# Projecting later images two units at a time: v's products 512 columns wide, q's and k's in longer runs

## The chip, the core and the metric

One Trainium2 chip, one core. The metric is the time of one launch on the device in microseconds, the median of several runs. The profile is of one further execution.

## The reference

A self-attention layer over each of 4 images of 64 x 64 places with 256 channels, in fp32:

```
N = W * H                                   # 4096
q = x Wq + bq    (128 channels)
k = x Wk + bk    (128 channels)
v = x Wv + bv    (256 channels)
pq = q.reshape(B, -1, N); pk = ...; pv = ...   # reshape, not transpose
energy = einsum('bcn,bcm->bnm', pq, pk)
attention = softmax(energy)
out = einsum('bcm,bnm->bcn', pv, attention).reshape(B, W, H, C)
return gamma * out + x
```

## The kernel before

TensorE multiplies in fp32r, and each operand is split into forms: an upper part `h`, the rest `l`, and a form `d` that makes up for the cross terms. A product is therefore three matmuls (forms 0, 1, 2) into one or two accumulators.

**Image 0** is projected at the start, unit by unit (16 units of 256 places). **The main loop** then runs over 512 steps `n`: 4 images x 8 groups (of 512 rows of the attention) x 16 steps `t` (of 256 columns each). In step `n` TensorE's instructions are laid out by hand, in this order:

- `cross(n + 2)`: two 512-column matmuls (L331), which ScalarE rescales in place (L332, "muls");
- `attend(n, 0)`: six 512-column matmuls (L403) into the accumulators `a0`, `b0`;
- `energy(n + 2)`: four matmuls (L346), followed by ScalarE's exponentials (L349) and its upper forms `h` (L355, in `upper`);
- a piece of the projection of the *next* image (`step(p, "pe")`);
- in the first step of a group, `sums`: two matmuls `z` (L441) for the softmax's sums of the group before;
- `attend(n, 1)`: six matmuls (L403) into `a1`, `b1`.

VectorE makes in each step the sum of the exponentials (L366) and the forms `l` and `d` (L380, L382, in `halves`). At a group's end `emptied` has ScalarE copy the accumulators into the tile `o` (L417): those of half 0 in the last step (t = 15), those of half 1 in the first step of the next group (t = 0), after that step's exponentials. `attend(n, 1)` of t = 0 starts to fill `a1` again, so it comes behind that copy. In the last image, which has no projection beside it, half 1 is emptied one step later (`late`) and two more PSUM banks are used.

`finish` ends a group in twelve pieces, one for each step (`proceed`): the sums go through DRAM and a reciprocal and come back as `r`, VectorE adds the two parts of `o` at t = 4 and multiplies by `r` at t = 7, GpSimd's queue adds `x` by DMA from t = 8, and SP's queue stores the result from t = 11.

The projection of the next image goes along in `step(p, engine)`, where `p` counts its own steps: `p = n - 4` at first, two of them in each step from n = 16 to 23, then `p = n + 4`. A unit has R = 8 steps `r`: transposes at r = 0 (four, L207), x's forms at 1 and 2 (L218, L220, L222), q's and k's products at r = 3 (four 256-column matmuls, L238) and 4 (eight), v's at 5 (four) and 6 (eight), the forms between and behind them (L260, L267, L278, L281, L155, L158). They use two PSUM banks in turn, which `z` uses too. The finished forms are stored to DRAM by SP's queue (`store`, L302), and come back by GpSimd's queue: `load_k` in every step, `load_v` for each of 16 steps around the change to the next image (768 KB each).

The SBUF pool `work` has tiles by tag: `xin` (one buffer) for the loaded x (`load_x`, L199), `xf` (one) for x's forms, `pf` (two in turn) for the forms of q, k and v until they are stored, `r` (one) for `zf` and `r`, `o` (one).

Of the kernel before, what the change touches and what calls it, by code (L numbers as in the profile page):

```python
# [9 lines left out]
F32 = mybir.dt.float32  # L10
F32R = mybir.dt.float32r
I32 = mybir.dt.int32
AF = mybir.ActivationFunctionType
# [7 lines left out]
def kernel(  # L21
# [36 lines left out]
    nc = tc.nc  # L58
    B, W, H, C = x.shape
    P = 128  # L60
# [3 lines left out]
    KC = C // P  # L64
    NI = NM // 2
# [9 lines left out]
    XB = 256  # L75
    xv = columns(x, XB)
# [4 lines left out]
    REST = 1.0 / (1.0 + E)  # L81
    NB = 512
    NJ = NB // P
    NG = N // NB
    NU = NM // 2
# [15 lines left out]
    with ExitStack() as fast:  # L101
# [22 lines left out]
        nc.scalar.dma_start(raw[:, 0, :, C2:], wk.rearrange("(k p) d -> p k d", p=P))  # L124
        nc.sync.dma_start(raw[:, 1], wv.rearrange("(k p) e -> p k e", p=P))
        nc.gpsimd.memset(zs, 1.0)
        bf = work.tile([P, 3, KC, 2, P], F32R, tag="xf", name="bf", bufs=1)
        bf = bf[:, 0, 0].rearrange("p s a -> p (s a)")
        rows = work.tile([P, 2, XB], F32, tag="xin", name="rows", bufs=1)[:33, 0]
        nc.vector.memset(rows, 0.0)  # L130
        for eh in range(KC):
            nc.gpsimd.dma_start(bvs[:, eh : eh + 1], bv[eh * P : (eh + 1) * P].unsqueeze(1))
# [56 lines left out]
            return pool.tile(shape, F32, tag=tag, name=name)  # L189

        def load_x(b, i):
            if i >= NI:
                return
            if b == 0:
                t = xs4[:, i % 4]
            else:
                t = work.tile([P, 2, XB], F32, tag="xin", name=f"x_{b}_{i}", bufs=1)
            if b or i:
                nc.sync.dma_start(t, xv[b, i])  # L199
            loads["x", b, i] = t  # L200

        def transposed(b, i):
            xs = loads.pop(("x", b, i))
# [5 lines left out]
        def x_forms(b, i):  # L209

            y = units.pop(("xt", b, i))
            if b == 0:
                f = ppool.tile([P, 3, KC, 2, P], F32R, tag="ld", name=f"xf_{b}_{i}")
            else:
                f = work.tile([P, 3, KC, 2, P], F32R, tag="xf", name=f"xf_{b}_{i}", bufs=1)
            units["xf", b, i] = f
            h = f[:, 0]
            nc.scalar.activation(h, y, AF.Identity, scale=UPPER)  # L218
            yield
            nc.vector.scalar_tensor_tensor(f[:, 2], h.bitcast(F32), 1.0 + E, y, ALU.mult, ALU.subtract)  # L220
            yield
            nc.vector.tensor_tensor(f[:, 1], y, h.bitcast(F32), ALU.subtract)  # L222
            yield

        def products(b, i, w, fs):
# [5 lines left out]
            for s in range(2):  # L231
                for f in fs:
                    for k in range(KC):
# [10 lines left out]
                            skip_group_check=True,  # L244
                        )

        def biased(i):

            to = units[0, 0, i]
            for s in range(2):  # L250
                nc.tensor.matmul(  # L251
                    to[:, s, :], ones_r, bf, start=False, stop=True, skip_group_check=True,
                )

        def seed_qk(b, i):
            y = units[0, b, i]
            if b == 0:
                nc.scalar.activation(y, y, AF.Identity, scale=REST)
                return
            nc.vector.scalar_tensor_tensor(  # L260
                y, y, REST, bias.unsqueeze(1).to_broadcast([P, 2, C]), ALU.mult, ALU.add
            )

        def seed_v(b, i):
            y = units[1, b, i]
            for eh in range(KC):
                nc.scalar.activation(  # L267
                    y[:, eh, :], y[:, eh, :], AF.Identity, bias=bvs[:, eh : eh + 1], scale=REST
                )

        def qk_forms(b, i):
            y = units.pop((0, b, i)).rearrange("p s (w a) -> p s w a", w=2)
# [13 lines left out]
                stores.append((kf[b, i // 2 + NU // 2 * s][:, i % 2], f[:, s, 1]))  # L286
                stores.append((qd[b, i // NJ + NG // 2 * s][:, i % NJ], f[:, s, 0]))

        def v_forms(b, i):
            y = units.pop((1, b, i))  # L290
            units.pop(("xf", b, i))
            if b == 0:
                f = vall[:, i]
            else:
                f = work.tile([P, 3, 2, C], F32R, tag="pf", name=f"vf_{b}_{i}")
            yield from split(f[:, 0], f[:, 1], f[:, 2], y)
            if b:
                stores.append((vf[b, i], f))

        def store():  # L300
            for to, f in stores:
# [122 lines left out]
        def sum_forms(n):  # L424

            s = now["total"] = now["sum"]
            f = work.tile([P, 2, NB], F32R, tag="r", name=f"zf_{n // NU}", bufs=1)
            h, l = now["z"] = f[:, 0, :], f[:, 1, :]
            nc.scalar.activation(h, s[:, 0, :], AF.Identity, scale=UPPER)
            yield  # L430
            nc.vector.tensor_tensor(l, s[:, 0, :], h.bitcast(F32), ALU.subtract)
            yield
# [11 lines left out]
        def finish(n, o, s):  # L444
            b, g = divmod(n, NG)
            r4 = rall[:, n, :]
            row = lambda t: t[n : n + 1, :]
            spread = lambda t: row(t).rearrange("o (p j) -> (o p) j", j=NJ)
            nc.sync.dma_start(row(zd), s[0:1, 0, :])
            yield  # L450
            nc.sync.dma_start(r4, spread(zd))
            yield
            yield
            nc.vector.reciprocal(r4, r4)
            yield
            nc.sync.dma_start(spread(rd), r4)
            nc.vector.tensor_tensor(o[:, 0], o[:, 0], o[:, 1], ALU.add)
            yield
            r = work.tile([P, NB], F32, tag="r", name=f"r_{n}", bufs=1)
            nc.sync.dma_start(r, rd[n, :].partition_broadcast(P))  # L460
            yield
            yield
            nc.vector.tensor_tensor(
                o[:, 0], o[:, 0], r.unsqueeze(1).to_broadcast([P, 2, NB]), ALU.mult
            )
            yield
            nc.gpsimd.dma_start(o[:, 0], xg[b, g], accum_op=ALU.add)
            yield
            yield
            yield  # L470
            nc.sync.dma_start(og[b, g], o[:, 0])
# [6 lines left out]
        def finish_last(n, xr):  # L478

            b, g = B - 1, NG - 1  # L480
            S = now["sum"][:, 0, :]
            f = work.tile([P, 2, NB], F32R, tag="r", name="zf_last", bufs=1)
            nc.scalar.activation(f[:, 0, :], S, AF.Identity, scale=UPPER)
            nc.vector.tensor_tensor(f[:, 1, :], S, f[:, 0, :].bitcast(F32), ALU.subtract)
            attend(n, 0)
# [41 lines left out]
            nc.sync.dma_start(og[b, g][:, 1], xr[:, 1, :])  # L527


        R = STEPS // NI  # L530

        def step(n, engine):

            if n < 0:
                return
            b, u = divmod(n, STEPS)
            i, r = divmod(u, R)
            b += 1
            made = now["made"]
            if engine == "pe" and b < B:  # L540
                if r == 0:
                    transposed(b, i)
                elif r == 3:
                    products(b, i, 0, (2,))
                elif r == 4:
                    products(b, i, 0, (0, 1))
                elif r == 5:
                    products(b, i, 1, (2,))
                elif r == 6:
                    products(b, i, 1, (0, 1))  # L550
            elif engine == "act" and b < B:
                if r == 1:
                    made["x"] = x_forms(b, i)
                    next(made["x"])
                    load_x(b, i + 1)
                elif r == 5:
                    made["qk"] = qk_forms(b, i)
                    next(made["qk"])
                elif r == 6:
                    seed_v(b, i)  # L560
                elif r == 7:
                    made["v"] = v_forms(b, i)
                    next(made["v"])
            elif engine == "dve":
                if r == 0 and "v" in made:
                    for _ in made.pop("v"):
                        pass
                if b < B:
                    if r in (1, 2):
                        next(made["x"])  # L570
                    elif r == 3:
                        seed_qk(b, i)
                    elif r == 5:
                        next(made["qk"])
                    elif r == 6:
                        for _ in made.pop("qk"):
                            pass
                    elif r == 7:
                        next(made["v"])

        now["made"] = {}
        now["turn"], now["banks"] = 0, [(ps_p, "p0"), (ps_p, "p1")]
# [32 lines left out]
        for i in range(NI):  # L615
# [3 lines left out]
            next(qk)  # L619
            if i == 0:  # L620
                products(0, 0, 1, (2,))
                seed_v(0, 0)
                products(0, 1, 0, (2,))
                seed_qk(0, 1)
            products(0, i, 1, (0, 1))
            vs = v_forms(0, i)
            next(vs)
            xs = iter(())
            if i + 1 < NI:
                if i:  # L630
                    products(0, i + 1, 0, (2,))
                    seed_qk(0, i + 1)
                products(0, i + 1, 1, (2,))
                seed_v(0, i + 1)
            if i + 2 < NI:
                transposed(0, i + 2)
                xs = x_forms(0, i + 2)
# [20 lines left out]
        for n in range(B * STEPS):  # L658
# [5 lines left out]
                load_x(1, 0)  # L664
            if u == STEPS - 5 and b + 2 < B:
                image(b + 2)
                load_x(b + 2, 0)
            if n == B * STEPS - 6:
                xr = ppool.tile([P, 2, NB], F32, tag="s", name="xr")
                nc.sync.dma_start(xr, xg[b, g])  # L670
# [4 lines left out]
            if turn:  # L675
                zf = sum_forms(n)
                next(zf)
            p = n - 4 if n < 16 else 2 * n - 20 if n < 24 else n + 4
            step(p, "act")
            if not final:  # L680
                attend(n, 0)
# [22 lines left out]
                break  # L704
            attend(n, 1)
            full = now["a", 1], now["b", 1]
            if 16 <= n < 24:
                for engine in ("act", "pe", "dve"):
                    step(p + 1, engine)
            if t == 6 and n + NU < B * STEPS:  # L710
# [221 lines left out]
```

## Time and profile before

| | |
|---|---|
| median of 3 runs | 2358.28 us (2358.22 to 2358.36) |
| the profiled execution | 2358.95 us, its span 2357.1 us |
| granted TensorE clock | 0.999 |
| busy: TensorE / VectorE / ScalarE | 99% / 91% / 80% |
| DMA | 413.82 MB, mean 176 GB/s |
| one group of 16 steps, images 0 to 2 | 72.8 us |

PE is TensorE's matmul, PEld its weight load, DVE VectorE, ACT ScalarE, POOL GpSimd, SP the queue of stores and of x's loads. Busy times of single matmuls overlap. `out<-in` names the tiles that an instruction writes and reads; a note in brackets tells how long the engine was idle before it and what released it.

### The profile page before, as it was taken

The numbers are of one execution on the slowest core, as the hardware profiler recorded it, in microseconds if no ns is written. First come the engines' busy times: TensorE is split into PE (matmuls) and PEld (weight loads), VectorE is DVE, ScalarE is ACT, GpSimd is POOL, SyncE is SP. The second block draws the span as 40 slices with busy tenths as digits, with TensorE's granted clock in tenths as the row PEclk, the third lists the DMA queues.
The fourth block names the chain that finished last, engine by engine and source line by source line (L and its number), as shares of the span: only waits on it lengthen the run. The fifth ranks groups of instructions, "written<-read, shape, count | busy, mean of one in ns | idle before, by whom it ended". The sixth has DMA issues, their size and how long they took to land.

```text
span 2357.1 us, 32019 instructions
## 1 busy us (share of the span) xinstructions
PE 2343.1 (99%) x11132; PEld 1958.5 (83%) x11132; DVE 2135.7 (91%) x2114; ACT 1878.8 (80%) x3090; POOL 355.7 (15%) x642
## 2 busy tenths in 40 slices
PE   9999999999999999999999999999999999999998
PEld 9888888888888888888888888888888888888886
DVE  8989999989999899999999999999989888888888
ACT  7788778888788887888878888778887777888785
POOL 1111111111211111111121111111112111111110
PEclk9999999999999999999999999999999999999999
DMA  8556665556975556556597555665559554444443
GB/s 281 153 161 176 177 172 159 166 158 175 305 240 173 149 174 188 162 159 165 154 344 223 161 166 157 178 173 159 172 152 353 159 134 121 121 130 118 130 130 96
DMA packets 178894, 413.82 MB, mean 176 GB/s; under 512 B 26083, under 2 KB 76519, under 8 KB 178726
## 3 DMA queue, kind: packets, MB, share of 16 engines
q0 software_dynamic: 94272, 280.67, 45.4%
q1 hardware_dynamic: 83902, 130.77, 15.4%
q8 instruction: 91, 1.49, 0.3%
q14 instruction: 77, 0.63, 0.1%
q10 hardware_dynamic: 552, 0.26, 0.0%
HBM read 306.64 MB, written 104.98 MB: 175 GB/s over the span
## 4 chain that ended last, share of the span: by engine, by line
PE 97%; ACT 1%; DVE 1%; issue 0%; DMA 0%; POOL 0%; ACTq 0%; DVEq 0%; POOLq 0%; SPq 0%
PE a L403 39%; PE e L346 20%; PE b L403 19%; PE e L331 10%; PE qv L238 7%; PE xt L207 1%; PE z L441 1%; ACT x L349 0%; ACT o L417 0%; DMA bias<-in_L_conv_bk_dram 0%; ACT e L332 0%; DVE f L281 0%; ACT h L355 0%; PE qv L251 0%; DVE v L158 0%
## 5 line engine op out<-in xcount | busy, mean ns | idle before, releaser
L349 ACT ACTIVATE x<-e 128x512 f32<-128x512 f32 x960 | 522.1, 596 | 295.5 <-PE e L346 289.0
L366 DVE TENSOR_TENSOR s<-s,x 128x1024 f32<-128x1024 f32 x480 | 586.7, 1222 | 94.6 <-ACT x L349 92.1
L380 DVE TENSOR_TENSOR ld<-x,h 128x1024 fp32r<-128x1024 f32 x480 | 586.3, 1221 | 87.3 <-ACT h L355 57.8
L403 PE MATMUL a<-h,v 128*128 128x512 f32 x2048 | 641.0, 394 | 0.0
L332 ACT ACTIVATE e<-e 128x512 f32<-128x512 f32 x1024 | 546.8, 573 | 109.1 <-PE e L331 108.7
L403 PE MATMUL a<-ld,v 128*128 128x512 f32 x2048 | 632.8, 390 | 0.0
L403 PE MATMUL b<-ld,v 128*128 128x512 f32 x2048 | 631.7, 390 | 0.2
L382 DVE SCALAR_TENSOR_TENSOR ld<-h,x 128x1024 fp32r<-128x1024 f32 x480 | 584.9, 1219 | 0.0
L318 POOL DMA_DIRECT2D k<-kf x512 | 272.1, 531 | 1942.4 <-PE e L346 1826.2
L346 PE MATMUL e<-q,k 128*128 128x512 f32 x2048 | 548.8, 390 | 1.1
L355 ACT ACTIVATE h<-x 128x1024 fp32r<-128x1024 f32 x480 | 510.6, 1064 | 13.2
L403 PEld LDWEIGHTS a<-ld,v 128*128 128x128 f32 x2048 | 384.4, 188 | 83.2
L403 PEld LDWEIGHTS b<-ld,v 128*128 128x128 f32 x2048 | 384.1, 188 | 83.5 <-DVE ld L382 1.0
L346 PEld LDWEIGHTS e<-q,k 128*128 128x128 f32 x2048 | 383.0, 188 | 84.5 <-ACT e L332 6.0
L403 PEld LDWEIGHTS a<-h,v 128*128 128x128 f32 x2048 | 368.6, 189 | 69.4 <-ACT o L417 7.3
L331 PE MATMUL e<-q,k 128*128 128x512 f32 x1024 | 316.1, 390 | 0.0
L331 PEld LDWEIGHTS e<-q,k 128*128 128x128 f32 x1024 | 191.7, 188 | 40.5
L238 PEld LDWEIGHTS qv<-wf,xf 128*128 128x128 f32 x768 | 108.5, 193 | 10.7 <-DVE xf L220 1.8
L238 PE MATMUL qv<-wf,xf 128*128 128x256 f32 x768 | 115.3, 287 | 1.6 <-DVE xf L220 1.4
L238 PEld LDWEIGHTS qv<-xf,wf 128*128 128x128 f32 x768 | 107.1, 191 | 8.6 <-ACT s L442 0.7
L238 PE MATMUL qv<-xf,wf 128*128 128x256 f32 x768 | 112.6, 283 | 0.5 <-ACT s L442 0.3
L281 DVE SCALAR_TENSOR_TENSOR f<-f,qv 128x512 fp32r<-128x512 f32 x128 | 85.8, 681 | 3.6 <-ACT f L278 3.1
(83 smaller groups left out, 1006.6 us busy)
## 6 DMA issues: line engine op xcount, KB each, us to landing
k<-kf POOLq DMA_DIRECT2D x512, 384.0 KB, 3.6
vf<-vf SPq DMA_DIRECT2D x48, 768.0 KB
v<-vf POOLq DMA_DIRECT2D x48, 768.0 KB, 8.1
kf<-f SPq DMA_DIRECT2D x128, 192.0 KB
qd<-f SPq DMA_DIRECT2D x128, 192.0 KB
q<-qd POOLq DMA_DIRECT2D x31, 768.0 KB, 4.8
o<-in_x_dram POOLq DMA_DIRECT2D x31, 512.0 KB, 7.3
out_dram<-o SPq DMA_DIRECT2D x31, 512.0 KB
```

The lines of the kernel that those rows point to most:

```text
L238: nc.tensor.matmul(to[:, s, :], left, right.rearrange("p s a -> p (s a)") if w else right, start=(f == 2 and s == k == 0), stop=(f == 1 an ...
L281: nc.vector.scalar_tensor_tensor(f[:, :, :, j, :], h.bitcast(F32), s, y, ALU.mult, op)
L318: nc.gpsimd.dma_start(t, kf[b, u % NU])
L331: nc.tensor.matmul(e, *forms(n, i, 2), start=True, stop=False, skip_group_check=True)
L332: nc.scalar.mul(e, e, -REST)
L346: nc.tensor.matmul(e, *forms(n, i, f), start=False, stop=(f == 1), skip_group_check=True)
L349: nc.scalar.activation(x[:, i, :], e, AF.Exp, scale=(1.0 + E) ** 3 / E)
L355: nc.scalar.activation(h, units[n], AF.Identity, scale=UPPER)
L366: nc.vector.tensor_tensor(s, s, x, ALU.add)
L380: nc.vector.tensor_tensor(l, x, h.bitcast(F32), ALU.subtract)
L382: nc.vector.scalar_tensor_tensor(d, h.bitcast(F32), 1.0 + E, x, ALU.mult, ALU.subtract)
L403: nc.tensor.matmul(to, vall[:, t, f, i, j * P : (j + 1) * P], units[n][f][:, i, :], start=(t == 0 and i == 0 and f != 1), stop=(t == NU - ...
```

## The change

Images 1 to 3 are projected by pairs of units. R becomes 16 steps per pair, and the steps are laid out anew:

- r = 0: the transposes of both units (eight); r = 1 to 4: x's forms of both, written side by side into one `xf` tile of double size;
- r = 5: the first four products of q and k of both units; r = 6: the other eight of both; their seeds on VectorE at r = 5, their forms at r = 7 to 10;
- r = 9 and 10: v's products of the first half of the channels, for both units at once, 512 columns wide (`products_v`: two matmuls at r = 9, four at r = 10); r = 11 and 12: the second half; seeds on ScalarE at r = 10 and 12, one of 512 columns each (`seed_v_pair`), forms at r = 11 to 14 (`v_pair_forms`), each stored with two DMAs;
- r = 15: both units of the next pair of x are loaded, with two DMAs.

`p = n - 3` at first, two of them in each step from n = 17 to 22, then `p = n + 3`. The tags `xin` and `r` go: the pair of x and `zf` take places in the ring `pf`, and `r` is loaded into the half of `o` that is free by then. The main loop's other calls stand as they were.

```diff
         def load_x(b, i):
...
+            pair = work.tile([P, 2, 2, XB], F32, tag="pf", name=f"x_{b}_{i}")
+            for u in range(2):
+                nc.sync.dma_start(pair[:, u], xv[b, i + u])
+                loads["x", b, i + u] = pair[:, u]
...
+        def products_v(b, i, eh, fs):
+            xf = units["xp", b, i]
+            if fs[0] == 2:
+                units["v", b, i, eh] = bank(f"v{eh}_{b}_{i}", [P, 2, C], b, 1)
+            to = units["v", b, i, eh]
+            for f in fs:
+                for k in range(KC):
+                    nc.tensor.matmul(
+                        to.rearrange("p u c -> p (u c)"),
+                        wf[:, 1, f, k, eh * P : (eh + 1) * P],
+                        xf[:, f, k].rearrange("p u s a -> p (u s a)"),
+                        start=(f == 2 and k == 0),
+                        stop=(f == 1 and k == KC - 1),
+                        skip_group_check=True,
+                    )
...
+        def seed_v_pair(b, i, eh):
+            y = units["v", b, i, eh]
+            nc.scalar.activation(y, y, AF.Identity, bias=bvs[:, eh : eh + 1], scale=REST)
...
+        def v_pair_forms(b, i, eh):
+            y = units.pop(("v", b, i, eh))
+            f = work.tile([P, 3, 2, C], F32R, tag="pf", name=f"vf{eh}_{b}_{i}")
             yield from split(f[:, 0], f[:, 1], f[:, 2], y)
+            for u in range(2):
+                stores.append((vf[b, i + u][:, :, eh, :], f[:, :, u, :]))
...
-            f = work.tile([P, 2, NB], F32R, tag="r", name=f"zf_{n // NU}", bufs=1)
+            f = work.tile([P, 2, NB], F32R, tag="pf", name=f"zf_{n // NU}")
...
-            r = work.tile([P, NB], F32, tag="r", name=f"r_{n}", bufs=1)
+            r = o[:, 1, 0]
...
-        R = STEPS // NI
+        R = 2 * STEPS // NI
...
+            if engine == "pe":
                 if r == 0:
                     transposed(b, i)
-                elif r == 3:
+                    transposed(b, i + 1)
+                elif r == 5:
                     products(b, i, 0, (2,))
-                elif r == 4:
+                    products(b, i + 1, 0, (2,))
+                elif r == 6:
                     products(b, i, 0, (0, 1))
+                    products(b, i + 1, 0, (0, 1))
+                elif r in (9, 11):
+                    products_v(b, i, r // 11, (2,))
+                elif r in (10, 12):
+                    products_v(b, i, r // 12, (0, 1))
+            elif engine == "act":
+                if r in (1, 2):
+                    begin(("x", r - 1), x_forms(b, i + r - 1))
+                elif r in (7, 8):
+                    begin(("qk", r - 7), qk_forms(b, i + r - 7))
+                elif r in (10, 12):
+                    seed_v_pair(b, i, r // 12)
+                elif r in (11, 13):
+                    begin(("v", r // 13), v_pair_forms(b, i, r // 13))
+                elif r == 15:
+                    load_x(b + (i + 2) // NI, (i + 2) % NI)
+            else:
+                if 1 <= r <= 4:
+                    next(made["x", (r - 1) // 2])
                 elif r == 5:
...
+                elif 7 <= r <= 10:
+                    next(made["qk", (r - 7) // 2])
...
+                elif 11 <= r <= 14:
+                    next(made["v", (r - 11) // 2])
...
-            p = n - 4 if n < 16 else 2 * n - 20 if n < 24 else n + 4
+            p = n - 3 if n < 17 else 2 * n - 20 if n < 23 else n + 3
...
-            if 16 <= n < 24:
+            if 17 <= n < 23:
                 for engine in ("act", "pe", "dve"):
                     step(p + 1, engine)
```

More of the change, by code (lines that the diff above doesn't have):

```diff
@@ L126 @@
         nc.gpsimd.memset(zs, 1.0)
-        bf = work.tile([P, 3, KC, 2, P], F32R, tag="xf", name="bf", bufs=1)
-        bf = bf[:, 0, 0].rearrange("p s a -> p (s a)")
-        rows = work.tile([P, 2, XB], F32, tag="xin", name="rows", bufs=1)[:33, 0]
+        bf = work.tile([P, 3, KC, 2, 2, P], F32R, tag="xf", name="bf", bufs=1)
+        bf = bf[:, 0, 0, 0].rearrange("p s a -> p (s a)")
+        rows = work.tile([P, 2, XB], F32, tag="pf", name="rows")[:33, 0]
         nc.vector.memset(rows, 0.0)
@@ L191, in load_x @@
         def load_x(b, i):
-            if i >= NI:
+            if b == B or i >= NI:
                 return
@@ L195, in load_x @@
                 t = xs4[:, i % 4]
[L196 to L200, printed above, removed]
+                if i:
+                    nc.sync.dma_start(t, xv[b, i])
+                loads["x", b, i] = t
+                return
+            pair = work.tile([P, 2, 2, XB], F32, tag="pf", name=f"x_{b}_{i}")
+            for u in range(2):
+                nc.sync.dma_start(pair[:, u], xv[b, i + u])
+                loads["x", b, i + u] = pair[:, u]
         def transposed(b, i):
@@ L213, in x_forms @@
                 f = ppool.tile([P, 3, KC, 2, P], F32R, tag="ld", name=f"xf_{b}_{i}")
+            elif i % 2 == 0:
+                f = units["xp", b, i] = work.tile(
+                    [P, 3, KC, 2, 2, P], F32R, tag="xf", name=f"xf_{b}_{i}", bufs=1
+                )
+                f = f[:, :, :, 0]
             else:
-                f = work.tile([P, 3, KC, 2, P], F32R, tag="xf", name=f"xf_{b}_{i}", bufs=1)
+                f = units["xp", b, i - 1][:, :, :, 1]
             units["xf", b, i] = f
@@ L245, in products @@
                         )
+        def products_v(b, i, eh, fs):
[12 more added lines that the diff above has]
+                        skip_group_check=True,
+                    )
         def biased(i):
@@ L262, in seed_qk, with seed_v @@
             )
-        def seed_v(b, i):
-            y = units[1, b, i]
+        def seed_v(i):
+            y = units[1, 0, i]
             for eh in range(KC):
@@ L287, in qk_forms, with v_forms @@
                 stores.append((qd[b, i // NJ + NG // 2 * s][:, i % NJ], f[:, s, 0]))
[L289 to L295, printed above, removed]
+        def v_forms(i):
+            y = units.pop((1, 0, i))
+            units.pop(("xf", 0, i))
+            yield from split(vall[:, i, 0], vall[:, i, 1], vall[:, i, 2], y)
+        def v_pair_forms(b, i, eh):
+            y = units.pop(("v", b, i, eh))
+            f = work.tile([P, 3, 2, C], F32R, tag="pf", name=f"vf{eh}_{b}_{i}")
             yield from split(f[:, 0], f[:, 1], f[:, 2], y)
-            if b:
-                stores.append((vf[b, i], f))
+            for u in range(2):
+                stores.append((vf[b, i + u][:, :, eh, :], f[:, :, u, :]))
         def store():
@@ L481, in finish_last @@
             S = now["sum"][:, 0, :]
-            f = work.tile([P, 2, NB], F32R, tag="r", name="zf_last", bufs=1)
+            f = work.tile([P, 2, NB], F32R, tag="pf", name="zf_last")
             nc.scalar.activation(f[:, 0, :], S, AF.Identity, scale=UPPER)
@@ L537, in step, with begin @@
             i, r = divmod(u, R)
-            b += 1
+            b, i = b + 1, 2 * i
+            if b >= B:
+                return
             made = now["made"]
-            if engine == "pe" and b < B:
+            def begin(key, pieces):
+                made[key] = pieces
+                next(pieces)
+            if engine == "pe":
                 if r == 0:
                     transposed(b, i)
-                elif r == 3:
+                    transposed(b, i + 1)
+                elif r == 5:
@@ L544, in step @@
                     products(b, i, 0, (2,))
-                elif r == 4:
+                    products(b, i + 1, 0, (2,))
+                elif r == 6:
                     products(b, i, 0, (0, 1))
-                elif r == 5:
[L548 to L579, printed above, removed]
@@ new lines, in step @@
+                    products(b, i + 1, 0, (0, 1))
[17 more added lines that the diff above has]
+                    next(made["x", (r - 1) // 2])
+                elif r == 5:
+                    seed_qk(b, i)
+                    seed_qk(b, i + 1)
+                elif 7 <= r <= 10:
+                    next(made["qk", (r - 7) // 2])
+                    if r % 2 == 0:
+                        next(made["qk", (r - 7) // 2], None)
+                elif 11 <= r <= 14:
+                    next(made["v", (r - 11) // 2])
+                    if r % 2 == 0:
+                        next(made["v", (r - 11) // 2], None)
@@ L621 @@
                 products(0, 0, 1, (2,))
-                seed_v(0, 0)
+                seed_v(0)
                 products(0, 1, 0, (2,))
@@ L625 @@
             products(0, i, 1, (0, 1))
-            vs = v_forms(0, i)
+            vs = v_forms(i)
             next(vs)
@@ L633 @@
                 products(0, i + 1, 1, (2,))
-                seed_v(0, i + 1)
+                seed_v(i + 1)
             if i + 2 < NI:
@@ L666 @@
                 image(b + 2)
-                load_x(b + 2, 0)
             if n == B * STEPS - 6:
```

## The prediction

> **What bounds the kernel now.** I read the page first: busy times, then the chain that ended last.
>
> ```profile
> span 2357.1 us, 32019 instructions
> PE 2343.1 (99%) x11132; PEld 1958.5 (83%) x11132; DVE 2135.7 (91%) x2114; ACT 1878.8 (80%) x3090; POOL 355.7 (15%) x642
> PE 97%; ACT 1%; DVE 1%; issue 0%; DMA 0%; POOL 0%; ACTq 0%; DVEq 0%; POOLq 0%; SPq 0%
> L403 PEld LDWEIGHTS a<-h,v 128*128 128x128 f32 x2048 | 368.6, 189 | 69.4 <-ACT o L417 7.3
> ```
>
> TensorE is the bound from end to end, so a change pays only if it shortens TensorE's stream or its waits, and every new wait of TensorE is paid in full. The last line is the one to remember: weight loads of the attention products sat idle until ScalarE's copies out of the accumulators (L417) had ended, 7.3 us in all. The list of that line's waits says 23 times, 0.32 us each: once at nearly every group start. The timeline of one such start (step 48, whose `cross` begins at 290.55):
>
> ```profile
> 287.78 1.07 PE L346 MATMUL e<-q,k 128*128 128x512 f32 x4
> 288.43 1.09 ACT L349 ACTIVATE x<-e 128x512 f32<-128x512 f32 x2 [0.38 <-PE e L346]
> 289.97 0.70 ACT L417 ACTIVATE o<-b,gam 128x512 f32<-128x512 f32 x1
> 290.55 0.61 PE L331 MATMUL e<-q,k 128*128 128x512 f32 x2
> 290.97 1.07 ACT L332 ACTIVATE e<-e 128x512 f32<-128x512 f32 x2 [0.30 <-PE e L331]
> 292.36 1.07 PE L346 MATMUL e<-q,k 128*128 128x512 f32 x4
> 293.01 1.09 ACT L349 ACTIVATE x<-e 128x512 f32<-128x512 f32 x2
> 293.27 1.11 PE L238 MATMUL qv<-wf,xf 128*128 128x256 f32 x8
> 293.98 0.69 ACT L417 ACTIVATE o<-a,gam 128x512 f32<-128x512 f32 x1
> 294.22 0.63 PE L441 MATMUL z<-zf,ones 128*128 128x512 f32 x2
> 294.73 0.30 PEld L403 LDWEIGHTS a<-h,v 128*128 128x128 f32 x2 [0.32 <-ACT o L417]
> 295.30 0.62 PE L403 MATMUL a<-ld,v 128*128 128x512 f32 x2
> ```
>
> Busy times overlap (matmuls are pipelined), so I take start to start. Four 512-column matmuls take 0.91 us (292.36 to 293.27): 0.2275 each. Eight 256-column ones take 0.95 (293.27 to 294.22): 0.119 each. The second accumulator half `a1` can be written only when the copy that began at 293.98 has ended at 294.67. TensorE would have been there at 294.68 and, because the weight load also waited, its next pair began at 295.30 where 295.13 was due: 0.17 us paid. What nearly hides the copies is the eight projection products (0.95) and `z` (0.46) between `energy` and `attend(n, 1)`.
>
> **The change, part by part.**
>
> *v's products.* In images 1 to 3, 48 units x 12 products of 256 columns become 288 of 512. Each saves 2 x 0.119 - 0.2275 = 0.010 us: 2.9 us. (With single intervals from the trace, 120 and 227 ns, 13 ns and 3.7 us.) The Trainium skill, "TensorE: Matmul & The Clock Gate", section "Wait — 56ns, not 53.3ns?", puts the fixed cost of a warm matmul at about 2.5 ns. By that the merging would bring an estimated 288 x 2.5 ns = 0.7 us and the sum below would end 2.2 us higher; this trace shows 10 to 13 ns, and goes ahead of it.
>
> *Longer runs.* Four transposes and the return to attention products take 0.44 + 0.03 us in the chain (the row after them lasts 0.94, not 0.91). Two runs joined save that return once, about 0.03 x 24 = 0.8 us. Runs of q's and k's products show no such step (120 ns to the last), so joining them brings nothing. Part sum -3.7, bounds -2.9 and -5.
>
> *ScalarE and VectorE.* VectorE has the same 14 pieces per pair (0.61 us start to start, beside 3 x 1.135 in each step). The hand-set steps bunch them: two seeds in one step, `o`'s addition and multiplication beside q's and k's forms. I followed its lag through one group: at worst 2 us, and TensorE asks for `d` about 1.7 us after that; hidden, and with that cover gone it would be TensorE's wait. ScalarE has two seeds of 512 columns instead of four of 256 (0.47 each): less work, off the bound.
>
> *The phase.* This is the large term. Before, step p = n + 4 of units of 8 puts eight products (r = 4) into every group's first step (t = 0) and four (r = 3) into the last. After, p = n + 3 of pairs of 16 puts t = 0 at r = 3, where TensorE has nothing to project, and t = 15 at r = 2, where TensorE has nothing either but ScalarE an x form more. The order of the built programs agrees: `energy`, the two `z` matmuls, `a1`. So at t = 0 the eight products no longer cover the copies. From the rows above: the last step is 0.48 shorter, so `cross` starts at 290.07. ScalarE's added x form (0.55 start to start) eats the 0.38 idle ahead of the exponentials, which start 0.10 late; half 0's copies end 290.77 with the next operation possible at 290.65, so L332 starts 0.16 later than TensorE would let it. From L332's start to the copy's it is 3.01 us (290.97 to 293.98), all back to back: copy from 293.66 to 294.35, weight load at 294.41, next pair 0.57 later (as 294.73 to 295.30): 294.98. TensorE's due time: 290.07 + 0.455 + 1.36 + 0.91 + 0.455 for the `a1` pair is 293.25, and 293.70 for the next. Paid: 1.28, against 0.17: 1.11 us more per group start. The groups that begin at n = 32, 48, ..., 368 are 22: **+24.4 us**. Lower bound: the exponentials are held by TensorE alone (second one ready 0.42 after the last `energy` start, as at 288.43): 0.87 each, 19.1. Upper: the x form finds no idle time and delays all by 0.39 more: 1.5 each, 33.0. I take the middle because the 0.38 of idle is in the row.
>
> *The start n = 16* falls on r = 13. There ScalarE must make v's `h` (L155) between L332 and the exponentials, in a `pf` buffer whose last store (first half of v) was made by VectorE only one step earlier, since `zf` now takes a place in the same ring of two. Store issue 0.5 each and some 4.5 us to land (the packets of v's store at 157.6 ended 4.2 after issue): about 2 us of wait plus 0.55, so 3.5 more, once; bounds 1 and 5.
>
> *SP's queue.* The pair of x is loaded at r = 15, one step before its transposes (before: seven steps), into the buffer that held the first half of v. The load waits in SP's queue for those stores, and behind `out`'s; v's second stores wait behind it. In an ordinary group: VectorE ends the piece 4 us into r = 12, stores land near 10, `out` is queued at 7, x lands at 12.5 to 15.5 (x's packets end 4.2 to 4.9 us after issue); the transposes come at 19.8. Hidden by 4 us. But at the turn to images 2 and 3 `load_v` fills the DMA engines:
>
> ```profile
> 620.00:640.00 20.00, 20.00 (x99) 16.84 (x99) 18.22 (x18) 14.88 (x25) 5.43 (x9) 1.00 1.09 342
> 640.61 0.55 SPq L199 DMA_DIRECT2D x<-in_x_dram  x1
> ```
>
> The DMA share is 1.09, and the x load of 640.61 had its last packet 8.0 us after issue, `out`'s at 633.6 11.3 us. With v's stores ahead x lands 22 to 23 us after r = 12 began: about 2.5 us late, twice: **+5**, bounds 0 and 12. v's stores in 1 KB runs instead of 6 KB cost the DMA engines 6 x 46 ns instead of 234; hidden outside those stretches.
>
> *Sum.* The profiled execution took 2358.95 us, 0.67 over the median of the runs. 2358.95 - 3.7 + 24.4 + 3.5 + 5 = 2388.2; less 0.67: **2387.5 us**.
>
> **Rivals.** (1) *The copies hide.* If the releaser named in that row is wrong, or ScalarE reaches the copies early enough that `a1` waits no longer than now, only the first term is left: 2358.3 - 3.7 = 2354.6, faster. It decides from 0.16 us more per start: below that, 23 waits cost less than 3.7. For it: TensorE's merged work is real. Against: 294.73 follows the copy's end by 0.06 us, 23 times over. (2) *x late at each pair.* If stores and `out` together take 6 us longer than I put, transposes wait 2 us at all 24 pairs: 48 more, about 2435. For it: one step of lead instead of seven. Against: margins of 4 us from measured landings. (3) *A draw*: rival 1 with waits of some 0.2 us, near 2358.
>
> **How the numbers follow.** Forecast 0.84, rival 1 0.05, rival 2 0.08, rival 3 0.03. The range takes in the forecast's bounds: 2358.3 + 19.1 + 1 - 5 = 2373 and 2358.3 + 33 + 5 + 12 - 2.9 = 2405, which would all have to fall together; I give 2372 to 2403, leaving the other cases out. A measurement tells 0.2% (4.7 us) from no change. Slower holds the forecast and rival 2: 0.92; same 0.03; faster 0.05.
>
> **What would show it.** In the changed profile the weight loads `a<-h,v` waiting for `o` should sum to some 25 to 35 us instead of 7.3, 23 times; the chain should show a piece of ScalarE at each group start 72 to 73 us apart. v's products should stand 0.227 apart. Transposes waiting for x should show at the two image turns only. I am wrong if a group (16 steps) from n = 32 on is not about 1 us longer than now.

## The result, and the profile after

The changed kernel takes 2398.39 us (median of 6 runs, 2396.61 to 2399.51), the kernel before 2358.43 beside it: ratio 1.0169, 95% interval 1.0158 to 1.018, some 40 us slower. The prediction was 2387.5, range 2372 to 2403. The profiled execution took 2396.61 us; its span is 37.6 us longer than that of before.

The page of the changed kernel, in answer to the four lines shown of before (lines move: 403 is now 433, 417 is 447, 331 is 361, 346 is 376, 441 is 471, 199 is 202):

```profile
span 2394.7 us, 31637 instructions
PE 2342.7 (98%) x10844; PEld 1948.1 (81%) x10844; DVE 2124.7 (89%) x2114; ACT 1858.6 (78%) x3042; POOL 355.8 (15%) x642
PE 86%; ACT 10%; DMA 1%; DVE 1%; issue 1%; SPq 0%; ACTq 0%; DVEq 0%
L433 PEld LDWEIGHTS a<-h,v 128*128 128x128 f32 x2048 | 378.7, 188 | 103.5 <-ACT o L447 30.8
```

ScalarE now holds 10% of the chain instead of 1%, and the weight loads that waited 7.3 us for the copies wait 30.8. That is 23 times, within the 25 to 35 us that the prediction named as its sign. Beside that there is a wait that before did not have at all. The waits of TensorE's matmuls, which are shorter than those of the weight loads ahead of them (what waited for what: us in all, times, longest):

```profile
PE a L433 <- ACT o L447: 20.7, 23, 2.6
PE xt L210 <- DMA x<-in_x_dram: 17.3, 4, 7.0
```

The group start that answers to the one shown of before, in the timeline of the changed kernel:

```profile
290.79 1.07 PE L376 MATMUL e<-q,k 128*128 128x512 f32 x4
290.96 0.59 ACT L226 ACTIVATE xf<-xt 128x512 fp32r<-128x512 f32 x1
291.44 1.09 ACT L379 ACTIVATE x<-e 128x512 f32<-128x512 f32 x2
293.06 0.62 PE L361 MATMUL e<-q,k 128*128 128x512 f32 x2
293.55 1.10 ACT L362 ACTIVATE e<-e 128x512 f32<-128x512 f32 x2
294.87 1.08 PE L376 MATMUL e<-q,k 128*128 128x512 f32 x4
295.52 1.09 ACT L379 ACTIVATE x<-e 128x512 f32<-128x512 f32 x2
295.78 0.63 PE L471 MATMUL z<-zf,ones 128*128 128x512 f32 x2
296.49 0.69 ACT L447 ACTIVATE o<-a,gam 128x512 f32<-128x512 f32 x1
297.24 0.30 PEld L433 LDWEIGHTS a<-h,v 128*128 128x128 f32 x2 [1.26 <-ACT o L447]
297.81 0.62 PE L433 MATMUL a<-ld,v 128*128 128x512 f32 x2
```

Nothing stands between `energy` (294.87) and `z` (295.78), and the weight load of `a1` waits 1.26 us for the copy that ends at 297.18. `a1`'s pair was due at 296.24 and the next at 296.69; that one starts at 297.81: 1.1 us paid instead of 0.17. Twenty-two group starts show the same: 0.98 us, to 0.02, beyond the due time between `z` and `a1`, and 0.12 behind it.

The second wait falls at the two image turns. The timeline of the first, and the busy time by stretch (columns: PE, PEld, DVE, ACT, POOL busy, granted clock, DMA share, GB/s):

```profile
648.77 1.07 PE L376 MATMUL e<-q,k 128*128 128x512 f32 x4
656.87 1.09 PE L210 MATMUL xt<-ident,x 128*128 128x128 f32 x4 [7.04 <-DMA x<-in_x_dram]
660.04 1.09 PE L210 MATMUL xt<-ident,x 128*128 128x128 f32 x4 [2.08 <-DMA x<-in_x_dram]
660.78 1.20 PE L433 MATMUL a<-h,v 128*128 128x512 f32 x2
661.78 1.05 PE L433 MATMUL a<-ld,v 128*128 128x512 f32 x2
```

```profile
640.00:650.00 10.00, 9.84 (x44) 7.81 (x42) 9.37 (x9) 7.14 (x13) 2.12 (x4) 1.00 1.10 396
650.00:661.00 11.00, 2.04 (x9) 1.70 (x10) 1.23 (x1) 1.56 (x3) 1.05 (x2) 0.59 0.98 352
661.00:665.00 4.00, 4.00 (x11) 3.13 (x11) 1.20 (x2) 0.84 (x2) 0.00 (x0) 0.50 0.01 4
665.00:670.00 5.00, 5.00 (x22) 4.04 (x22) 3.19 (x5) 3.74 (x7) 1.06 (x2) 0.94 0.23 51
```

The transposes wait 7.04 us for the first unit of x and 2.08 for the second (at the second turn 6.25 and 1.97), and the granted clock falls to 0.50 and stays there after TensorE is busy again: attention products take 0.86 us a pair (661.78 to 662.64) instead of 0.455. The step took 16.5 us (646.95 to 663.49 by its `cross`) where one with eight transposes takes 5.0, and the next lost 1 us more.

Where the 37.6 us went, by the starts of `cross`: an ordinary group of 16 steps from n = 32 on takes 73.41 us instead of 72.81. These 0.60 us are 0.93 at the group start (1.10 less 0.17), less 0.16 by the smaller number of matmuls and some 0.17 by smaller gaps between the others, whose cause stays open. Twenty-two groups make 13.3. The two turns add 12.6 and 10.9, and steps 0 to 31 add 2.7, about the one wait of 2.6 at n = 16. What stands ahead of step 0 and the last image, which the change hardly touches, came out 1.9 shorter in this execution.

### The profile page after: what moved, and what is told of

It is laid out like the page before. It is cut to its first block, busy times and chain, and to the rows that moved or that the text cites. A ratio compares the mean times of both kernels' runs of the same rounds, so it can differ in the third digit from the quotient of the medians.

```text
span 2394.7 us, 31637 instructions
## 1 busy us (share of the span) xinstructions
PE 2342.7 (98%) x10844; PEld 1948.1 (81%) x10844; DVE 2124.7 (89%) x2114; ACT 1858.6 (78%) x3042; POOL 355.8 (15%) x642
## 3 DMA queue, kind: packets, MB, share of 16 engines
q1 hardware_dynamic: 115390, 130.77, 15.8%
## 4 chain that ended last, share of the span: by engine, by line
PE 86%; ACT 10%; DMA 1%; DVE 1%; issue 1%; SPq 0%; ACTq 0%; DVEq 0%
PE a L433 35%; PE b L433 17%; PE e L376 17%; PE e L361 9%; PE qv L246 4%; PE v L263 3%; ACT x L379 2%; ACT o L447 2%; ACT h L385 2%; ACT e L362 2%; PE xt L210 1%; ACT s L379 1%; DMA x<-in_x_dram 1%; DMA vf<-vf 1%; ACT xf L226 1%
## 5 line engine op out<-in xcount | busy, mean ns | idle before, releaser
L433 PE MATMUL a<-h,v 128*128 128x512 f32 x2048 | 637.8, 393 | 20.7 <-ACT o L447 20.7
L385 ACT ACTIVATE h<-x 128x1024 fp32r<-128x1024 f32 x480 | 510.9, 1064 | 13.3
L433 PEld LDWEIGHTS a<-h,v 128*128 128x128 f32 x2048 | 378.7, 188 | 103.5 <-ACT o L447 30.8
L246 PE MATMUL qv<-wf,xf 128*128 128x256 f32 x768 | 107.5, 286 | 2.5 <-DVE xf L228 1.4
L246 PEld LDWEIGHTS qv<-wf,xf 128*128 128x128 f32 x768 | 101.8, 192 | 8.1 <-DVE xf L228 1.8
L263 PE MATMUL v<-xf,wf 128*128 128x512 f32 x288 | 81.0, 390 | 0.0
L410 DVE TENSOR_TENSOR ld<-s,h 128x1024 fp32r<-128x1024 f32 x32 | 39.2, 1226 | 29.5 <-ACT h L385 28.5
```

The lines of the kernel that those rows point to most:

```text
L246: nc.tensor.matmul(to[:, s, :], left, right.rearrange("p s a -> p (s a)") if w else right, start=(f == 2 and s == k == 0), stop=(f == 1 an ...
L263: nc.tensor.matmul(to.rearrange("p u c -> p (u c)"), wf[:, 1, f, k, eh * P : (eh + 1) * P], xf[:, f, k].rearrange("p u s a -> p (u s a)"), ...
L385: nc.scalar.activation(h, units[n], AF.Identity, scale=UPPER)
L410: nc.vector.tensor_tensor(l, x, h.bitcast(F32), ALU.subtract)
L433: nc.tensor.matmul(to, vall[:, t, f, i, j * P : (j + 1) * P], units[n][f][:, i, :], start=(t == 0 and i == 0 and f != 1), stop=(t == NU - ...
```

## The experiments

My theory: (a) the group starts lost their cover, (b) the turns lose to a late x, and the rest is a small gain. The main rival for (a): not the phase, but the pairs themselves (the x form moved to t = 15, the shared ring `pf`).

**1. The kernel before, with the phase alone.**

```diff
-            p = n - 4 if n < 16 else 2 * n - 20 if n < 24 else n + 4
+            p = n - 4 if n < 16 else 2 * n - 20 if n < 22 else n + 2
...
-            if 16 <= n < 24:
+            if 16 <= n < 22:
```

> The kernel before, with p = n + 2 instead of n + 4 from n = 22 on: a group's first step (t = 0) then stands at r = 2 of the unit, where TensorE has no products; nothing else changes. Theory (the lost cover): the wait of a1 for ScalarE's copies rises from 0.17 to about 1.1 us at 22 group starts, so the time is 20 to 24 us over the kernel before, 2378 to 2382. Rival (the loss at group starts comes from the pairs themselves: the x form moved to t = 15, the ring pf shared with zf and x): no change, 2358 to 2360.

Measured: 2380.24 us, ratio 1.0091 (1.0074 to 1.0108), 21.8 over the kernel before. Its waits, and two lines of a group start:

```profile
PE a L403 <- ACT o L417: 18.1, 22, 0.8
288.26 0.60 ACT L218 ACTIVATE xf<-xt 128x512 fp32r<-128x512 f32 x1
294.62 0.30 PEld L403 LDWEIGHTS a<-h,v 128*128 128x128 f32 x2 [1.26 <-ACT o L417]
```

The same weight load waits the same 1.26 us. The phase is the cause; neither the pairs nor the shared ring is needed for it. The edit does move more than TensorE's products, though: ScalarE's x form stands at t = 15 here too (288.26), so this run alone cannot part it from the lost cover. The rows can. The exponentials behind the x form start 0.65 us after `energy` in the changed kernel (290.79 to 291.44), as they did before (287.78 to 288.43): the x form fits into idle time. And at the group start the pair behind `a1` comes 0.95 us later after `z` than before (297.81 less 295.78, against 295.30 less 294.22), as much as the eight missing products took.

**2. The copies of half 1 on VectorE** (in the changed kernel, images 0 to 2):

```diff
+                from_ = banks[c] if banks else now["ab"[c], j]
+                if j and n + 1 < (B - 1) * STEPS:
+                    nc.vector.tensor_scalar(now["o"][:, c, j, :], from_, scale, None, ALU.mult)
+                    continue
```

> The changed kernel, with the copies of accumulator half 1 (images 0 to 2) made by VectorE, which idles 1.4 us there waiting for ScalarE's h, instead of ScalarE behind the exponentials. Theory: 22 waits of 1.1 us and the one of 2.8 at n = 16 go: 2398 - 27 = 2371, 2369 to 2375. Rival (VectorE, 89% busy, gives the time back: its forms come late to attend): 2380 to 2398, with TensorE waiting for ld.

Measured: 2372.91 us (2371.39 to 2374.79), 25.5 less than the changed kernel. No `a1` waits for a copy any more, and a group takes 72.35 us instead of 73.41; TensorE's longest waits are those for x (16.8 us in 4). VectorE did not become the bound.

**3. x into the free half of `o`, at r = 12.**

```diff
-            pair = work.tile([P, 2, 2, XB], F32, tag="pf", name=f"x_{b}_{i}")
+            if i + (b - 1) * NI > 2:
+                pair = now["o"][:, 1].rearrange("p u (s c) -> p u s c", s=2)
+            else:
+                pair = work.tile([P, 2, 2, XB], F32, tag="pf", name=f"x_{b}_{i}")
...
-                elif r == 15:
+                if r == (12 if n >= R else 15):
```

> The changed kernel, with each pair of x from the third on loaded at r = 12 into the half of o that is free from t = 8 to t = 14, instead of at r = 15 into the ring pf: no wait for v's stores, four steps of lead. Theory (the two image turns cost some 11 to 12 us each, by the chain of stores, out and x in SP's queue): 2398 - 23 = 2375, 2372 to 2379, and no transposes waiting. Rival (the DMA engines are simply full there and x comes late whenever it is asked for within the turn): 2386 to 2398.

Measured: 2377.39 us (2374.56 to 2378.79), 21.0 less. No transpose waits for x at the turns any more; the 20.7 us for the copies stand as they were.

**4. Both edits.**

> The changed kernel with both edits of the two runs before. Theory: what is left of the change is TensorE's 3.7 us, and the 0.17 us at 23 group starts that the kernel before pays go as well (3.9): 2358.4 - 7.6 = 2351, 2349 to 2354. Rival (the two stretches hide one another, or VectorE becomes the bound at group starts): 2358 or more.

Measured: 2351.15 us (2349.22 to 2353.2, 7 runs), ratio to the kernel before 0.9968 (0.9957 to 0.998): faster than both kernels. TensorE holds 96% of the chain again, and no wait of its matmuls is longer than 1.4 us.

**5. v's products cut back to 256 columns**, in the kernel with both edits:

```diff
+                    for u in range(2):
+                        nc.tensor.matmul(
+                            to[:, u, :],
+                            wf[:, 1, f, k, eh * P : (eh + 1) * P],
+                            xf[:, f, k, u].rearrange("p s a -> p (s a)"),
```

> The kernel with both edits (x in o, copies on VectorE), but v's products cut back to two matmuls of 256 columns each, one for each unit, in the same places. Theory (the trace's interval: 120 ns for 256 columns, 227 for 512): 288 x 13 ns = 3.7 us more than the kernel with both edits, 2354 to 2355.5. Rival (some 2.5 ns fixed cost per matmul): 0.7 us more, 2351.5 to 2352.5.

Measured: 2355.88 us (2355.42 to 2359.55, 11 runs), 4.7 more than with 512 columns: 16 ns for each of the 288 merged pairs. The two times come from two sets of runs, whose intervals together leave some 3 us open. The traces are sharper: six groups take 435.52 us against 434.08, which is 20 ns for each, or 5.8 us over 24 pairs. The matmul's own interval gives 13 of these; the rest lies in gaps of a few ns between attention products (`a<-h` to `a<-ld`, 1.8 against 0.7 ns on average), whose cause stays open.

**6. The kernel before, with only the copies on VectorE.**

> The kernel before, with only the copies of half 1 moved to VectorE. Theory: its own wait of 0.17 to 0.18 us at 23 group starts goes: 2358.4 - 4 = 2354.4, 2353.5 to 2355.5. Rival (VectorE's two copies make the forms late and cost TensorE as much): 2357.5 or more.

Measured: 2354.26 us (2353.23 to 2355.28, 11 runs), ratio 0.9982 (0.9973 to 0.9991): the 0.17 us at each start were real and go too. A group takes 72.63 us here; with pairs and products of 256 columns (run 5) it takes 72.59.

**7. v stored in runs of 3 KB** (in the changed kernel; the tiles of v's forms and `vall` have the channel half ahead of the form):

```diff
-            f = work.tile([P, 3, 2, C], F32R, tag="pf", name=f"vf{eh}_{b}_{i}")
+            f = work.tile([P, 2, 3, C], F32R, tag="pf", name=f"vf{eh}_{b}_{i}")
...
-                stores.append((vf[b, i + u][:, :, eh, :], f[:, :, u, :]))
+                stores.append((vf[b, i + u][:, eh], f[:, u]))
```

> The changed kernel, with the forms of v laid out so that its stores and loads move runs of 3 KB instead of 1 KB stores (and 6 KB loads); all else as it is. Theory A (the 1 KB runs make v's stores land 15 us after issue at the image turns): they land in 9 to 10 us, x comes 5 us earlier, twice, and the half-clock stretch behind it shrinks: 2383 to 2391. Theory B (the engines are full with load_v and load_k there, whatever the run's length): 2395 to 2400.

Measured: 2395.05 us (2393.73 to 2398.34). SP's queue around the turn, of the changed kernel and then of this one:

```profile
633.09 1.25 SPq L332 DMA_DIRECT2D vf<-vf  x2
639.83 0.54 SPq L501 DMA_DIRECT2D out_dram<-o  x1
648.94 1.25 SPq L202 DMA_DIRECT2D x<-in_x_dram  x2
```

```profile
635.64 0.80 SPq L332 DMA_DIRECT2D vf<-vf  x2
643.81 0.60 SPq L501 DMA_DIRECT2D out_dram<-o  x1
645.55 1.23 SPq L202 DMA_DIRECT2D x<-in_x_dram  x2
```

x is issued when v's stores have landed: 15.8 us after their issue with 1 KB runs, 9.9 with 3 KB. That half of theory A is right, but the time is only 3.3 us less, outside the range of theory A and just inside that of theory B: TensorE still waits 12.6 us for x at the turns, where it waited 17.3. In the packets of the trace x now stands behind `out`: issued at 645.55, it begins when the last packets of `out` end (651.7) and lands at 658.8.

**8. Both edits and 3 KB runs.**

> The kernel with both edits and the 3 KB runs. Both theories: no wait at the image turns is left to shorten, 2349 to 2352; if the longer runs of load_v (3 KB instead of 6 KB) load the DMA engines more, load_k comes late at the turns and it is 1 to 3 us slower.

Measured: 2353.8 us (2351.39 to 2356.24, 11 runs), no gain over the kernel with both edits. It is some 2.6 us behind by the medians of two sets of runs, whose intervals overlap (0.9969 to 0.9987, and 0.9957 to 0.998), so that a loss is not shown.

**9. x into `o`, but at r = 15 as in the changed kernel.**

> The changed kernel with the pairs of x in the free half of o, as in the run with r = 12, but loaded at r = 15 as in the changed kernel: the same lead of one step, without the wait for v's stores. Theory (the wait for v's stores, 15.8 us to land at the turn, is what makes x late): x is issued right behind out's store, 8 us earlier, and is late by 1 to 3 us at each turn: 2378 to 2384. Rival (one step of lead is too little at the turns, whatever stands before it): 2388 to 2397.

Measured: 2398.91 us (2397.45 to 2401.58). My theory fell. x no longer waits for v's stores and is issued at 643.74, right behind `out`, yet the chain of this run stands on it until 661.79:

```profile
643.74 0.60 SPq L205
644.38 17.41 DMA o<-in_x_dram
```

Counted from the first `cross` of its group, x is issued at 54.8 us instead of 62.3 and lands at 72.9 instead of 73.2: 7.4 us earlier in, 0.3 earlier out. What makes x late is the work ahead of it in the DMA engines, not the buffer. The packets of the changed kernel show the same: `out`'s end at 652.5 and x's begin at 652.7, though x was issued at 648.94.

**10. Without `load_v`.**

> The changed kernel, leaving out 15 of 16 load_v at each change of image, so that images 1 to 3 are attended with v of image 0 for those columns; the time is that of the same instructions otherwise. Theory (load_v fills the DMA engines, and only therefore stores, out and x take 10 to 16 us each): no transposes wait at the turns, the clock stays full, 2373 to 2378. Rival (the chain in SP's queue is too long by itself): some 6 us of wait remain at each turn, 2385 or more.

Measured: 2374.9 us (2373.3 to 2377.27). No transpose waits at the turns, the clock stays at 1.00 there, and the DMA share is 0.86 and then 0.60, where the changed kernel had 1.10 ahead of its wait:

```profile
620.00:640.00 20.00, 20.00 (x90) 16.53 (x89) 18.92 (x20) 15.97 (x27) 4.31 (x7) 1.00 0.86 247
640.00:660.00 20.00, 20.00 (x94) 16.66 (x93) 17.55 (x17) 15.86 (x27) 2.12 (x4) 1.00 0.60 185
```

So the turns are lost where a load with one step of lead meets full DMA engines. Either is enough to undo it: four steps of lead ahead of v's stores and `out` (run 3), or no `load_v` beside it (this run).

## Why the prediction was right, and where it was off

*v's products*: 2.9 us forecast, 3.7 by single intervals; run 5 gives 4.7 by time and 5.8 by the length of the groups. The term was too small: I priced the interval of the merged matmuls alone, and the gaps between other products shrank with them. The Trainium skill, "TensorE: Matmul & The Clock Gate", section "Wait — 56ns, not 53.3ns?", puts the fixed cost at 2.5 ns. By that an estimated 0.7 us would have come; run 5 decides for the trace.

*Longer runs*: 0.8 us forecast. The 72.63 and 72.59 us of runs 6 and 5 are 0.04 apart, 1.0 us over 24 pairs; the phase differs between the two as well, so this only agrees.

*The phase*: 1.11 us more per start forecast, 0.93 measured, 20.5 for 24.4. The mechanism was right, and runs 1 and 2 show it from both sides. Mis-sized was the delay of ScalarE: I had L332 0.58 us after `cross`, it was 0.49 (293.06 to 293.55), because the x form took 0.48 start to start (290.96 to 291.44) and not 0.55 and so delayed the exponentials not at all, where I had 0.10; and from L332 to the copy it was 2.94 instead of 3.01.

*n = 16*: 3.5 forecast, 2.6 in the one wait there, 2.7 over steps 0 to 31.

*The turns*: 5 forecast with bounds of 0 and 12, 23.5 measured. This is the step that failed, in size and in its reason. I took each landing from the trace of before, where 768 KB of v went in 6 KB runs and x was one load, and put them one behind the other. By that x was to land 22 to 23 us after r = 12 began; at the first turn it landed after 30.2 (629.73 to 659.91). v's stores took 15.8 us from issue, where some 10 were left for them beside the 4 for VectorE and the 8.0 for x, and both units of x then needed 11 more. I named the wait for v's stores as what gates x; run 9 shows that without that wait x comes just as late. And I did not price what a wait of 7 us does to the clock: about 2 us of each turn are matmuls at half speed.

That the total stayed in the range is partly luck. With the turns at 23.5 and the other terms as forecast it would have been 2387.5 + 18.5 = 2406, above the 2403 that I gave. The group starts came out 4 us lower, and the smaller gaps took off some 3 to 4 us that I had not counted on. The last sign that the prediction names tells the same: a group was to be about 1 us longer, and it is 0.60.

*Rival 1* needed waits of less than 0.16 us more per start: it was 0.93 more. *Rival 2*, x late at each pair, did not come: outside the turns no transpose waits, so the 4 us of cover held. It was right about the lead of one step, but only where the engines are full. *Rival 3*, a draw, went with rival 1.

## What to carry to other kernels

On an engine that is busy from end to end, work that stands between another engine's result and its use is also cover; before moving it, look for waits that are nearly zero and ask what hides them. A transfer's lead has to be judged at the most crowded moment of the kernel, by what stands ahead of it in the DMA engines, not by its usual landing time. And a wait found in this way may be cheap to remove at its source: copies moved to an engine that idles there gave 4 us to the kernel before as well.

## What the runs showed of the hardware

At the first turn of the changed kernel the granted clock fell to 0.50 at 651.9, 2.1 us after the last matmul ahead of the wait had ended (649.8). It came back at 665.6, about 5.5 us after TensorE was steadily busy again (660.0). The length of a wait does not settle it alone. The wait of 2.6 us at n = 16 left the clock at full in this profile, but in run 10 the same wait was followed by 3.4 us at half, by as much in runs 7 and 9, and by 6.8 us in run 3:

```profile
148.50:152.00 3.50, 3.50 (x10) 2.70 (x9) 1.49 (x3) 2.39 (x5) 0.00 (x0) 0.51 0.01 5
```

The waits of 0.82 us at the group starts never did it. The Trainium skill, "TensorE: Matmul & The Clock Gate", section "What's actually happening", tells of half rate after an idle window of some 3.4 us and of full rate after a busy one. The return agrees with that. The fall at 651.9 and those at n = 16 came after less idle time, 2.1 us and at most 2.7, and that goes ahead of the page.

With the DMA engines full, the queue with the smaller runs got the smaller share. Between 633 and 660 us of the changed kernel GpSimd's queue moved 7.41 MB and SP's only 2.61, in a like number of packets:

```profile
q0 software_dynamic: 1936, 7.41, 77.6%
q1 hardware_dynamic: 2392, 2.61, 31.1%
```

The Trainium skill, "DMA: Bandwidth & Descriptors", section "Queues, rings and completion order", says that an engine serves its queues in turn, a packet at a time. The like numbers of packets in these rows fit that; whether the page's packet is what the profile counts as one is not shown here. Run 7 points the same way: its stores in 3 KB runs landed in 9.9 us instead of 15.8, but it also cut the loads of v from 6 KB runs to 3 KB, and which of the two did it is open. That x's own runs of 1 KB kept run 7 from gaining more is only argued.

The weight load at the head of a wait was not made early: it began with its matmul (both at 297.24), and the next pair followed 0.57 us later (297.81) instead of 0.455, which adds 0.12 us to each such wait.
